# One graph-attention layer on one core: a quad's last gather issued first from the 17th quad on, carried rows added and divided later, and two operands moved between SBUF and PSUM

## The chip, the cores and the metric

The kernel runs on one core of one Trainium2 chip. The core has a tensor engine (PE, with its weight loads listed as PEld), a vector engine (DVE), a scalar engine (ACT), GpSimd (POOL, which also issues the indirect gathers) and a queue for plain transfers (SP). They run at the same time and wait for each other through semaphores. The time is the device time of one execution in microseconds; before the change it is 2001.82 us, the median of three runs (2001.02 to 2005.26).

## The reference

One layer of graph attention over 12500 nodes and 200000 edges, sorted by target node:

```
h = relu(layernorm(x)) @ W_node.T                      # 12500 x (4 heads x 32)
e = edge_attr @ W_edge.T                               # 200000 x (4 x 32)
att = leaky_relu(sum(concat(h[src], h[tgt], e) * a))   # one number per edge and head
m = max(segment_max(att, tgt), 0);  ex = exp(att - m[tgt])
denom = segment_sum(ex, tgt) + (num_edges - deg) * exp(-m)
out = x + segment_sum(ex / denom[tgt] * h[src], tgt)
```

Targets are skewed: many edges have a low target, few a high one, so equal numbers of edges cover few nodes at first and many later.

## The kernel before, in words

Edges are cut into 392 groups of 511, each held as four chunks of 128 rows with one place left over, chunk 0 row 0, for a sum carried in from the group before. Four groups are a quad (98 of them), and up to four quads a super. For each chunk POOL issues one indirect transfer (function `gather`, L180) that fetches 128 rows of 137 floats of a table of node values, made at the start, into the tile `ga`. `ga` holds eight quads, so the gathers of quad q overwrite the rows of quad q-8 and wait for its readers. There are 1566 gathers: 72 from the raw input at the start and 1494 from the table.

For each quad, `all_logits` compares targets with a range of nodes (DVE, tile `at`, L653 or L662), and multiplies edge features and target values into a bank `lg` (PE, L683 and L686). `add_sources` copies the sources' share out of the gathered rows (ACT, tile `U`, L730); it waits on a semaphore that counts the quad's gathers. Once a super is complete, `softmax` runs scans along its edges (DVE, L795 to L868, in the bank `t_ps`), which need a mask `kp` of edges that have the same target as the one before; `keeps` makes it on DVE (L763), from the targets `dr` and a copy of them that ACT puts into PSUM (L757, or L760 for the last super). Then `sums` goes over the quads one super behind: DVE multiplies `ga` by the weights (L1023, L1063) and marks rows in `hot` (L1006, L1065), and PE adds the rows up (L1093) into a bank `acc`, of which there are three.

Ranges of 4, 2 or 1 groups share one sum. For the first 75 quads (4 or 2), `passed_on` takes the last sum of the quad before along (DVE, L944, after an exponential on ACT, L938), `entered` adds carried rows into that quad's bank with a small matmul (PE, L963), and `settled` divides (`divide_ranges`, DVE, L1294 to L1303). From quad 75 on each group has its own sum: chunk 0 comes last, after the carried row (`carried_in`, ACT L916, PE L908), ACT copies the sum out (L976), and `divide` does it in SBUF (L1319 to L1333). The end of the program is an order by hand, `finale`: POOL takes over a few marks (L1002) and multiplications (L1023) once its gathers are issued, and one division is cut in two, the product (L1328) first and the addition of `x` (L1333) some steps later.

All engines keep the order in which this Python program records their instructions: generators advanced in turn (`together`, `chain`, `step`) write it, and nothing is moved by a scheduler. `checked` runs beside the sums: it looks whether the rows of targets are sorted, with four comparisons on DVE (L1467), each from SBUF and from a copy that ACT puts into PSUM (L1466).

Of the kernel before, what the change touches and what calls it, by code (L numbers as in the profile page):

```python
# [9 lines left out]
F32 = mybir.dt.float32  # L10
# [4 lines left out]
OP = mybir.AluOpType  # L15
# [54 lines left out]
def kernel(  # L70
# [100 lines left out]
    def gather(q, rows, width, lo, hi):  # L171

        g0, m = quads[q]
        ga = GA[q] = ga_all[:, q % QUADS]
        for i in range(lo, hi):
            n = -(-min(E - (g0 + i) * NE + 1, GE) // P)
            if n < J:
                nc.vector.memset(ga[:, i, n:, :], 0.0)
            for j in range(n):
                came = nc.gpsimd.indirect_dma_start(  # L180
                    out=ga[:, i, j, 0:width], out_offset=None, in_=rows,
                    in_offset=bass.IndirectOffsetOnAxis(ap=srci[:, g0 + i, j:j + 1], axis=0))
                if q >= QUADS:
                    came.then_inc(arrived[q % len(arrived)], 16)
                    tc.no_tile_sem_insts.add(came.ins.name)
                    tc.add_to_no_dep_group(f"rows{q}", came.ins)
                    landings[q] = landings.get(q, 0) + 16
# [354 lines left out]
    with tc.tile_pool(name="work", bufs=2) as work, \  # L542
# [52 lines left out]
        def fetch_windows(q):  # L595
# [5 lines left out]
                                rows_at(side, at[i], 2 * SIDE, span)) for i in range(n)]  # L601
# [146 lines left out]
        def keeps(s):  # L748
# [6 lines left out]
            if 0 < s < len(supers) - 1:  # L755
                before_ps = acc_pool.tile([P, GE], F32, name="acc")
# [172 lines left out]
        def passed_on(fc):  # L929
# [23 lines left out]
            state["passed"] = row, both, den[:1 + span, 0:n]  # L953

        def entered():
# [3 lines left out]
            (q, bank), (row, both, den) = state.pop("pending"), state.pop("passed")  # L959
# [76 lines left out]
        def sums(q):  # L1036
# [12 lines left out]
            k, span = class_of(q)  # L1049
            pt = work.tile([P, QG, ROW], F32, name="pt", bufs=3) if k == 1 else None  # L1050
# [21 lines left out]
            for i in range(m):  # L1072
# [10 lines left out]
                if not i:  # L1083
                    settled()
                if new:
# [4 lines left out]
                    fc = fac if g == s0 else None  # L1090
                least_j = 1 if k == 1 else 0
# [5 lines left out]
                if i == 1:  # L1097
                    passed_on(fac if g0 == s0 else None)
                if i == (2 if k > 1 else 1):
# [208 lines left out]
        def divide(q, pt, den, lo, hi, since, whole=True):  # L1308
# [16 lines left out]
            if not lo:  # L1325
                RES[q] = work.tile([P, QG, D], F32, name="res")
            res = RES[q][:R, lo:hi]
            nc.vector.tensor_tensor(  # L1328
                res[:, :n, :].rearrange("p g (h d) -> p g h d", d=HD), val[:, :, :, 0:HD],
                share_ps[0:R, :n, :].unsqueeze(3).to_broadcast([R, n, H, HD]), op=OP.mult)  # L1330

            def added():
                nc.vector.tensor_tensor(res[:, :n, :], res[:, :n, :], xw, op=OP.add)  # L1333
# [485 lines left out]
```

## Time and profile before

| | |
|---|---|
| median of 3 runs | 2001.82 us (2001.02 to 2005.26) |
| profiled execution | 2001.54 us, its span 1999.8 us |
| POOL | busy 1496.3 us (75%), of which 1566 gathers |
| DVE | busy 1199.0 us (60%) |
| PE / PEld | busy 1111.8 us (56%) / 762.8 us (38%) |
| ACT | busy 325.2 us (16%) |
| granted TensorE clock | 0.750 of full speed on average |
| HBM | 210.74 MB read, 17.43 MB written |

In the profile's rows a group stands as line, engine, operation, output<-input, then shapes and count; behind the bar its busy time and the mean of one in ns, then the idle time of the engine just ahead of it and what ended that. "issue" is time in which the engine waited for nothing that the profile shows. A row of the timeline begins with the start and the duration in us. A row of waits has the time in total, how often, and the longest.

### The profile page before, as it was taken

To read this page: it belongs to the slowest core of one execution; us is meant where nothing else is said; L and a number is where in the kernel's file an instruction comes from. 1 tells how busy PE (TensorE), PEld (TensorE's weight loads), DVE (VectorE), ACT (ScalarE), POOL (GpSimd) and SP (SyncE) were. 2 spreads that over 40 slices of the span, in tenths; PEclk is the share of its full clock that TensorE was granted. 3 is DMA by queue.
4 is the path that set the end of the run, shared out by engine and by line. 5 is a ranking of instruction groups with operands and counts; after the bars stand their busy time and mean duration, and the time that the engine had idled before them with its cause. 6 is when DMAs were issued, how large, how long until landed. Compare 5 with 4: busy or idle time off the path is not lost. (4 is left out here: it accounts for less than half of the span.)

```text
span 1999.8 us, 18826 instructions
## 1 busy us (share of the span) xinstructions
PE 1111.8 (56%) x5116; PEld 762.8 (38%) x5116; DVE 1199.0 (60%) x2695; ACT 325.2 (16%) x1081; POOL 1496.3 (75%) x1596
## 2 busy tenths in 40 slices
PE   6567676456364564554645635546446365465666
PEld 4445444334243342342433424424334233234344
DVE  8675888356265464563754735636547356366676
ACT  6564111001001010110010100100101011122222
POOL 7777777777777777777777777777777777777774
PEclk9788788677686776776867867768677667677777
DMA  7754755344343443444435434444354343434431
GB/s 253 207 134 98 175 134 137 75 107 109 97 111 91 119 108 96 114 104 117 118 85 130 115 90 118 106 115 118 86 127 109 85 119 98 122 98 115 111 98 40
DMA packets 167749, 229.58 MB, mean 115 GB/s; under 512 B 60827, under 2 KB 100669, under 8 KB 167638
## 3 DMA queue, kind: packets, MB, share of 16 engines
q0 software_dynamic: 50112, 109.61, 24.2%
q1 hardware_dynamic: 115824, 116.14, 20.4%
q10 hardware_dynamic: 1702, 2.59, 0.4%
q8 instruction: 41, 0.67, 0.1%
q14 instruction: 70, 0.57, 0.1%
HBM read 210.74 MB, written 17.43 MB: 114 GB/s over the span
## 5 line engine op out<-in xcount | busy, mean ns | idle before, releaser
L180 POOL DMA_INDIRECT ga<-table,srci x1494 | 1412.8, 946 | 457.0 <-issue 430.1
L1093 PEld LDWEIGHTS acc<-ga,hot 128*113 128x113 f32 (+1 forms) x2928 | 468.3, 207 | 548.7 <-issue 296.7
L1093 PE MATMUL acc<-ga,hot 128*113 128x137 f32 (+1 forms) x2928 | 528.6, 337 | 188.6 <-DVE hot L1065 43.6
L686 PE MATMUL lg<-at,pw 112*96 112x512 bf16 (+2 forms) x392 | 151.1, 423 | 247.0 <-DVE at L653 235.6
L683 PE MATMUL lg<-ea,by_pair 128*96 128x512 f32 (+1 forms) x392 | 243.1, 706 | 11.9 <-ACT tg L696 11.9
L653 DVE TENSOR_TENSOR at<-const_ps,db 112x1024 bf16<-112x1024 f32 (+1 forms) x176 | 212.5, 1208 | 6.1 <-DMA db<-offset 6.1
L763 DVE TENSOR_TENSOR kp<-dr,acc 64x512 f32<-64x512 int32 (+3 forms) x26 | 17.1, 659 | 300.5 <-ACT acc L757 300.5
L944 DVE SCALAR_TENSOR_TENSOR pt<-pt,spare,acc 1x133 f32<-1x133 f32 x113 | 38.0, 337 | 243.8 <-ACT den_of L938 242.4
L1063 DVE TENSOR_TENSOR ga<-ga,ex_ps 128x1056 f32<-128x1056 f32 x147 | 181.6, 1235 | 0.0
L787 PE MATMUL t_ps<-ident,U 128*64 128x128 f32 (+2 forms) x210 | 46.0, 389 | 216.3 <-ACT den_of L938 192.3
L730 ACT COPY U<-ga 128x64 f32<-128x64 f32 x98 | 29.0, 297 | 832.3 <-DMA ga<-table,srci 832.3
L1065 DVE TENSOR_TENSOR hot<-const_ps,slot 128x896 f32<-128x896 f32 (+1 forms) x147 | 143.3, 975 | 0.0
L787 PEld LDWEIGHTS t_ps<-ident,U 128*64 128x64 f32 (+2 forms) x210 | 36.5, 197 | 240.9 <-ACT den_of L938 208.3
L878 PE MATMUL ex_ps<-ident,stack 128*128 128x128 f32 x105 | 28.9, 428 | 156.4 <-DVE stack L868 138.7
L686 PEld LDWEIGHTS <-pw 112*96 112x96 bf16 (+2 forms) x392 | 53.8, 137 | 104.3 <-issue 100.4
L180 POOL DMA_INDIRECT ga<-in_x_dram,srci x72 | 68.3, 948 | 23.1 <-issue 18.6
L1023 DVE TENSOR_TENSOR ga<-ga,ex_ps 128x528 f32<-128x528 f32 x92 | 63.5, 693 | 36.4 <-ACT xs L884 36.3
L878 PEld LDWEIGHTS ex_ps<-ident,stack 128*128 128x128 f32 x105 | 18.6, 215 | 170.5 <-ACT stack L866 170.5
L683 PEld LDWEIGHTS lg<-ea,by_pair 128*96 128x96 f32 (+1 forms) x392 | 63.1, 192 | 34.3 <-issue 17.2
L712 PE MATMUL t_ps<-tg,of_head 96*64 96x512 f32 (+3 forms) x96 | 59.2, 703 | 3.4 <-ACT tg L696 3.4
L976 ACT COPY pt<-acc 81x137 f32<-81x137 f32 x88 | 23.7, 269 | 168.3 <-PE acc L908 166.2
L908 PE MATMUL acc<-ga,hot 128*81 128x137 f32 x176 | 44.4, 342 | 11.7 <-ACT ga L916 9.2
(204 smaller groups left out, 1278.3 us busy)
## 6 DMA issues: line engine op xcount, KB each, us to landing
ea<-in_edge_t_dram SPq DMA_DIRECT2D x196, 256.0 KB
ga<-table,srci POOLq DMA_INDIRECT x1494
db<-offset SPq DMA_DIRECT2D x53, 256.0 KB
db<-in_dst_dram SPq DMA_DIRECT2D x20, 320.0 KB
db<-offset SPq DMA_DIRECT2D x35, 160.0 KB
table<-row SPq DMA_DIRECT2D x9, 616.5 KB
xt<-in_x_dram SPq DMA_DIRECT2D x9, 576.0 KB
inputs<-in_x_dram SPq DMA_DIRECT2D x92, 56.0 KB
```

What stands on the lines that cost most here:

```text
L180: came = nc.gpsimd.indirect_dma_start(out=ga[:, i, j, 0:width], out_offset=None, in_=rows, in_offset=bass.IndirectOffsetOnAxis(ap=srci[:, ...
L653: nc.vector.tensor_tensor(AT[q][:span, i:i + n, :].rearrange("p g e -> p (g e)"), part_ps[:span].to_broadcast([span, n * GE]), DB[q][:span ...
L683: nc.tensor.matmul(lg, by_pair[:, begin:begin + n], ea[:, i // 2, :], start=half == 0 and i == 0, stop=False, skip_group_check=True)
L686: nc.tensor.matmul(lg, PW[q][:span, begin:begin + n], at[:span, i, :], start=False, stop=full and i == quads[q][1] - 1, skip_group_check=True)
L712: nc.tensor.matmul(TP[s][:groups(s)[1] * H], of_head[supers[s][1], p][:n], tg[:n], start=p == 0, stop=False, skip_group_check=True)
L787: nc.tensor.matmul(t_ps[:R, j * P:(j + 1) * P], u[:, j, :R], ident, start=False, stop=j == C - 1, skip_group_check=True)
L878: nc.tensor.transpose(turned_ps[:, j, :], stack[:, j * P:(j + 1) * P], ident)
L908: nc.tensor.matmul(acc, hot[:, i, 0, 0:acc.shape[0]], ga[:, i, 0, :], start=False, stop=stop)
L1023: engine.tensor_tensor(val, val, weight.unsqueeze(3).to_broadcast([P, J, H, HW]), op=OP.mult)
L1063: nc.vector.tensor_tensor(val, val, weight.unsqueeze(3).to_broadcast([P, TWO * J, H, HW]), op=OP.mult)
L1065: nc.vector.tensor_tensor(hot[:, i:i + TWO, :, 1:1 + span].rearrange("p g j c -> p (g j) c"), lane_ps[:, 0:span].unsqueeze(1).to_broadcast ...
L1093: nc.tensor.matmul(acc, hot[:, i, j, 0:1 + span], ga[:, i, j, :], start=new and j == J - 1 and not second, stop=k > 1 and i % k == k - 1 a ...
```

## The change

Eight edits, the line numbers below being those of the kernel before:

- `gather`: from quad 16 on, chunk 0 of the quad's last group is issued first, the others in the old order.
- `fetch_windows`: the weights of a quad are queued on SP from the last range to the first.
- `keeps`: the copy for the mask goes to the bank `t_ps`, no longer to one of the three `acc` banks; in `all_logits` a super of more than two quads makes its mask in its second quad, after the last group, where it was in its last quad, after the first group.
- `passed_on` and `entered`: from quad 8 to quad 74 the passing moves from after the second group to after the third; the division of the quad before stands right behind it (it was ahead of the first group), and the small matmuls stand ahead of the fourth group's matmuls (they were behind the third's).
- `divide`: where product and addition are apart (once, in `finale`), the product goes to the bank `lg` instead of the SBUF tile `res`.
- `checked`: the copy into PSUM is gone, and DVE compares two SBUF rows.

```diff
@@ gather
-        for i in range(lo, hi):
-            n = -(-min(E - (g0 + i) * NE + 1, GE) // P)
...
-            for j in range(n):
-                came = nc.gpsimd.indirect_dma_start(
...
+        order = [(i, j) for i in range(lo, hi) for j in range(chunks(i))]
+        if q >= 2 * QUADS:
+            order.sort(key=lambda at: at != (hi - 1, 0))
+        for i, j in order:
+            came = nc.gpsimd.indirect_dma_start(
...
@@ fetch_windows
-                                rows_at(side, at[i], 2 * SIDE, span)) for i in range(n)]
+                                rows_at(side, at[i], 2 * SIDE, span)) for i in range(n)[::-1]]
@@ keeps
-                before_ps = acc_pool.tile([P, GE], F32, name="acc")
+                before_ps = ps.tile([P, GE], F32, name="t_ps")
@@ passed_on / entered
-            state["passed"] = row, both, den[:1 + span, 0:n]
+            state["passed"] = state.pop("pending") + (row, both, den[:1 + span, 0:n])
...
-            (q, bank), (row, both, den) = state.pop("pending"), state.pop("passed")
+            q, bank, row, both, den = state.pop("passed")
@@ sums
+            later = k > 1 and q >= QUADS
...
-                if not i:
+                if not i and not later:
+                    entered()
                     settled()
...
+                if later and i == m - 1:
+                    entered()
...
-                if i == 1:
+                if i == (2 if later else 1):
                     passed_on(fac if g0 == s0 else None)
-                if i == (2 if k > 1 else 1):
+                    if later:
+                        settled()
+                if not later and i == (2 if k > 1 else 1):
                     entered()
@@ divide
+            product = res if whole else ps.tile([P, GE], F32, name="lg").rearrange(
+                "p (g d) -> p g d", d=D)[:R]
             nc.vector.tensor_tensor(
-                res[:, :n, :].rearrange("p g (h d) -> p g h d", d=HD), val[:, :, :, 0:HD],
+                product[:, :n, :].rearrange("p g (h d) -> p g h d", d=HD), val[:, :, :, 0:HD],
...
-                nc.vector.tensor_tensor(res[:, :n, :], res[:, :n, :], xw, op=OP.add)
+                nc.vector.tensor_tensor(res[:, :n, :], product[:, :n, :], xw, op=OP.add)
@@ all_logits
-                if i == 0 and q == sum(supers[of_quad[q]]) - 1 and q < first_fold:
+                q0, n = supers[of_quad[q]]
+                if i == (QG - 1 if n > 2 else 0) and q == q0 + min(1, n - 1) and q < first_fold:
                     keeps(of_quad[q])
@@ checked
-                rows_ps = acc_pool.tile([P, 512], F32, name="acc")[:n, 0:NE]
-                nc.scalar.copy(rows_ps, rows[:n, 0:NE])
-                nc.vector.tensor_tensor(falls[:n], rows[:n, 1:NE + 1], rows_ps, op=OP.is_lt)
+                nc.vector.tensor_tensor(falls[:n], rows[:n, 1:NE + 1], rows[:n, 0:NE],
+                                        op=OP.is_lt)
```

POOL around the end of quad 15 and the whole of quad 16, with the semaphores that each gather waits for (an engine's name is that engine's counter, DMASW that of an earlier gather), before:

```order
L180 DMA ga<-table,srci 128x137 [waits DMASW7_49]
L180 DMA ga<-table,srci 128x137 [waits DVE_49,PE_49,Activation_49]
L180 DMA ga<-table,srci 128x137 x3
L180 DMA ga<-table,srci 128x137 [waits DVE_49,PE_49]
L180 DMA ga<-table,srci 128x137 x3
```

and of the change, from the last four gathers of quad 15:

```order
L183 DMA ga<-table,srci 128x137 [waits DMASW4_49,DVE_49,PE_49]
L183 DMA ga<-table,srci 128x137 [waits DMASW5_49]
L183 DMA ga<-table,srci 128x137 [waits DMASW6_49]
L183 DMA ga<-table,srci 128x137 [waits DMASW7_49]
L183 DMA ga<-table,srci 128x137 [waits DVE_49,PE_49,Activation_49]
L183 DMA ga<-table,srci 128x137 x15
```

Before, the first gather of each group of four had waits of its own; now the first gather of the quad has them all, and fifteen follow without a wait.

PE in the middle of the program, at a quad with ranges of two groups (L1093 and L1100 are the sums, L963 and L966 the small matmuls that add carried rows, `lg` and `t_ps` the logits and selections of a later quad), before:

```order
L1093 MATMUL acc<-ga,hot 113x137 x4
L963 MATMUL acc<-pt,spare 2x133 x2
L683 MATMUL lg<-ea,by_pair 96x512
L686 LDWEIGHTS pw
L686 MATMUL lg<-at,pw 96x512
L712 MATMUL t_ps<-tg,of_head_0_102 64x512
L1093 MATMUL acc<-ga,hot 113x137 x4
```

and now:

```order
L1100 MATMUL acc<-ga,hot 113x137 x4
L686 MATMUL lg<-ea,by_pair 96x512
L689 LDWEIGHTS pw
L689 MATMUL lg<-at,pw 96x512
L715 MATMUL t_ps<-tg,of_head_0_102 64x512
L966 MATMUL acc<-pt,spare 2x133 x2
L1100 MATMUL acc<-ga,hot 113x137 x4
```

The two small matmuls went from behind the third group's sums, past the logits, to just ahead of the fourth group's.

DVE in `finale`, from the reciprocal of the cut division on, before:

```order
L1324 RECIPROCAL const_ps<-den 81x16
L1328 TENSOR_TENSOR res<-pt,const_ps 81x512
L883 MEMSET xs 128x4x8
L763 TENSOR_TENSOR kp<-dr,const_ps 64x129
L1023 TENSOR_TENSOR ga<-ga,ex_ps 128x4x132 x2
L918 TENSOR_TENSOR ga<-acc,fac 1x132
L1333 TENSOR_TENSOR res<-res,inputs 81x512
L795 TENSOR_TENSOR t_ps<-t_ps,low 64x128
```

and now:

```order
L1333 RECIPROCAL const_ps<-den 81x16
L1339 TENSOR_TENSOR lg<-pt,const_ps 81x512
L886 MEMSET xs 128x4x8
L766 TENSOR_TENSOR kp<-dr,const_ps 64x129
L1026 TENSOR_TENSOR ga<-ga,ex_ps 128x4x132 x2
L921 TENSOR_TENSOR ga<-acc,fac 1x132
L1344 TENSOR_TENSOR res<-lg,inputs 81x512
L798 TENSOR_TENSOR t_ps<-t_ps,low 64x128
```

The order is the same; the product now stands in PSUM (`lg`), and the addition reads one operand from there and one from SBUF, where it read two from SBUF.

19 lines of the change are left out of this document (10 added, 9 removed).

## The prediction

> **What bounds the kernel now.** I read the shares of the engines first, then what POOL waited for, then the last stretch engine by engine.
>
> ```profile
> PE 1111.8 (56%) x5116; PEld 762.8 (38%) x5116; DVE 1199.0 (60%) x2695; ACT 325.2 (16%) x1081; POOL 1496.3 (75%) x1596
> L180 POOL DMA_INDIRECT ga<-table,srci x1494 | 1412.8, 946 | 457.0 <-issue 430.1
> L180 POOL DMA_INDIRECT ga<-in_x_dram,srci x72 | 68.3, 948 | 23.1 <-issue 18.6
> POOL ga L180 <- issue: 448.7, 1471, 0.6
> POOL ga L180 <- PE acc L1093: 4.0, 13, 0.3
> ACT U L730 <- DMA ga<-table,srci: 832.3, 73, 19.4
> 3.00:1962.70 1959.70, 1089.40 (x4989) 743.48 (x4989) 1172.87 (x2609) 316.11 (x1040) 1481.08 (x1566) 0.75 0.46 117
> 1962.70:1999.80 37.10, 22.38 (x127) 19.33 (x127) 24.27 (x73) 9.12 (x41) 14.28 (x23) 0.73 0.09 22
> ```
>
> 75% looks like slack, but the idle time of POOL is issue time: 448.7 us over 1471 gaps is 0.305 us each, the longest 0.6. A gather takes 0.946 us, and 0.946 + 0.305 = 1.251; 1566 times that is 1959 us, the whole stretch from 3.0 to 1962.7 (the two window rows: length, then PE, PEld, DVE, ACT, POOL busy). So up to 1962.7 the time is a count of gathers, and everybody else waits: ACT alone stood 832.3 us before a quad's rows had landed. What can move the end is (a) a stall put into POOL's row of gathers, (b) a gather made longer, (c) the 37.1 us behind the last gather.
>
> **The change, part by part.**
>
> *Fewer waits on POOL, 0.* The gathers are as many. A gap ended by PE is 4.0/13 = 0.31 us, one by issue alone 0.305: the waits lie inside the gap. Even 0.005 us at each of the some 250 places that lose a wait would be 1 us. I take 0.
>
> *The new first gather waits for the last group of the quad eight before, 0.* Until now its own group, read first, was enough. The room left:
>
> ```profile
> 298.33 1.16 PE L1093 MATMUL acc<-ga,hot 128*81 128x137 f32 x8
> 325.55 0.94 POOL L180 DMA_INDIRECT ga<-table,srci  x1 [0.30 <-issue]
> 1035.38 1.10 PE L1093 MATMUL acc<-ga,hot 128*113 128x137 f32 x8
> 1084.55 0.94 POOL L180 DMA_INDIRECT ga<-table,srci  x1 [0.31 <-issue]
> ```
>
> Quad 8's last matmuls end at 299.5, quad 16's first gather goes out at 325.5: 26 us. In mid-program (quad 46, then quad 54) it is 1084.55 - 1036.48 = 48 us. The second pair is typical, the first the tightest of those reordered; no stall.
>
> *Carried rows later, division later, mask earlier, weights reversed: 0.* The same instructions in another order. The passing still stands on DVE behind ACT's exponential, which stands behind a copy `U` that waits for rows; queued behind it are DVE's weights and PE's fourth group. What covers that:
>
> ```profile
> 1164.50:1244.40 79.90, 41.98 (x192) 29.33 (x192) 45.12 (x85) 6.86 (x24) 60.39 (x65) 0.73 0.44 109
> DVE kp L763 <- ACT acc L757: 300.5, 23, 17.9
> DVE pt L944 <- ACT den_of L938: 242.4, 30, 13.6
> ```
>
> One super is 64 gathers, 79.9 us, in which DVE works 45 and PE 42. The 300.5 and 242.4 us that DVE stands before mask and passing are idle time of an engine that waits for gathers anyway; an earlier mask shortens that, and what is late next is again the gather. Without that cover the whole 543 us would count; with it none does. The edits end with quad 74 (mask and waits apart), 23 quads before the end, so they don't reach the last stretch.
>
> *Two SBUF operands in the sorting check, +0.6 us.* Four comparisons lose the copy in PSUM. A row of that kind, the addition L1333 next to the gathers:
>
> ```profile
> 1621.06 0.69 DVE L1333 TENSOR_TENSOR res<-res,inputs 81x512 f32<-81x512 f32 x1
> 1620.07 0.95 POOL L180 DMA_INDIRECT ga<-table,srci  x1 [0.30 <-issue]
> 1621.32 1.25 POOL L180 DMA_INDIRECT ga<-table,srci  x1 [0.30 <-issue]
> ```
>
> The gather beside it took 1.25 instead of 0.95: 0.3 us on the chain that sets the end. Not every one is hit, so I take half, 0.15 each, 0.6 in all; bounds 0 and 4 x 0.3 = 1.2. The Trainium skill ("SBUF — State Buffer", Who interferes with whom) infers that descriptor generation needs the write side of the port shared with GpSimd and a two-input operation only its read side. By that rule the term is 0 and the sum 0.6 lower; this row speaks for a small cost. The four copies saved on ACT are worth nothing (ACT is 16% busy).
>
> *The product in PSUM, in the last stretch, -2.8 us.* Here lies the one large number:
>
> ```profile
> 1966.90 0.27 DVE L918 TENSOR_TENSOR ga<-acc,fac 1x132 f32<-1x132 f32 x1
> 1967.10 5.35 DVE L1333 TENSOR_TENSOR res<-res,inputs 81x512 f32<-81x512 f32 x1
> 1972.38 0.28 DVE L795 TENSOR_TENSOR t_ps<-t_ps,low 64x128 f32<-64x128 f32 x1
> 1973.15 0.42 DVE L801 TENSOR_TENSOR_SCAN t_ps<-kp,t_ps 64x128 f32<-64x128 f32 x1
> 1973.90 0.21 DVE L806 COPY two<-t_ps 64x1 f32<-64x1 f32 x2 [0.32 <-ACT low L804]
> 1962.75 3.72 POOL L1002 TENSOR_SCALAR hot<-lane,slot 128x80 f32<-128x80 f32 x8
> 1966.45 5.28 POOL L1023 TENSOR_TENSOR ga<-ga,xe 128x528 f32<-128x528 f32 x5
> 1971.72 4.19 POOL L1002 TENSOR_SCALAR hot<-lane,slot 128x80 f32<-128x80 f32 x8
> 1966.61 0.27 ACT L792 ACTIVATE low<-t_ps 64x128 f32<-64x128 f32 x1 [0.94 <-PE t_ps L787]
> 1970.67 0.27 ACT L976 COPY pt<-acc 81x137 f32<-81x137 f32 x1 [3.26 <-PE acc L908]
> 1973.61 0.26 ACT L804 COPY low<-t_ps 64x128 f32<-64x128 f32 x1 [2.67 <-DVE t_ps L801]
> 1967.14 3.03 PE L1093 MATMUL acc<-ga,hot 128*81 128x137 f32 x12 [0.58 <-ACT ga L1034]
> 1969.97 0.67 PE L908 MATMUL acc<-ga,hot 128*81 128x137 f32 x2
> 1975.46 1.66 PE L1093 MATMUL acc<-ga,hot 128*81 128x137 f32 x6 [4.83 <-DVE ga L1023]
> ```
>
> The addition L1333 takes 0.69 elsewhere and 5.35 here, and it ends 0.7 after POOL's five multiplications, which also read two SBUF operands: DVE was shut out for all five, 4.66 us. L918 beside it, one operand from PSUM, took its 0.27. With `lg` in PSUM the addition takes 0.69 and L795, whose `low` was there at 1966.88, starts at 1967.8. But the 4.66 don't reach the end. The scans end 4.6 earlier, at 1968.9; next is ACT's copy L804, and on ACT it is queued behind L976, which waits for PE's L908 until 1970.64. L976 starts at 1970.67, and copies follow each other some 0.17 apart, so L804 runs at 1970.84 to 1971.1 and DVE's L806 at 1971.13 instead of 1973.90: **2.77 us**. From there the order stands as before: L806 leads to DVE's weights (L1023), these to PE at 1975.46, and on through the last softmax to the end; POOL's marks, over at some 1975.4, are not asked for in that stretch. So the term is -2.77. Bounds: -4.58 if ACT were not held by L976, and -2.3, if the small SBUF copies that now fall beside L1002 give back a whole mark of 3.72/8 = 0.47.
>
> **Sum:** -2.77 + 0.6 = -2.2. The profiled execution ran 2001.54 us around its span of 1999.8, which gives 1999.4; it stands 0.3 below the median shown, so on the median's scale **1999.6 us**, 0.1% less.
>
> **Rivals.**
>
> *Clock (faster, 1998.2).* PE stands idle for 4.83 us before 1975.46, and the next three batches run at half clock:
>
> ```profile
> 1960.93:1971.17 10.24, 6.66 (x26) 5.23 (x26) 9.68 (x16) 2.46 (x10) 9.90 (x15) 0.50 0.10 22
> 1971.17:1974.58 3.41, 0.00 (x0) 0.00 (x0) 2.95 (x8) 0.42 (x2) 3.41 (x7) 1.00 0.05 12
> 1974.58:1981.41 6.83, 5.38 (x23) 4.97 (x24) 5.67 (x29) 2.24 (x11) 1.97 (x4) 0.50 0.07 18
> ```
>
> The granted clock (third number from the end) was full just while PE had nothing to do, then half again. With PE back at 1972.7 the idle time is 2.1 us, and the clock may stay. The first batch, 1.66 + 0.67 us, would then halve, ACT's queue opens 1 us sooner, a later batch gives 0.4: -1.4 more. The Trainium skill ("TensorE: Matmul & The Clock Gate", What's actually happening) has the gate look at windows of about 3.4 us that run free of the program: the same lengths as these rows, and by it the phase, so luck, decides.
>
> *The stall only moves (no change, 2002.0).* Another chain of the last stretch, PE with ACT's carried copies, sets the end, or the sorting check takes its full 1.2. For it: PE is busy 22 of 37 us there. Against: its batches at 1975.46 start on DVE's word.
>
> *The reordered wait reaches POOL (slower).* One late group now holds all sixteen gathers. It decides once the sums fall 48 us behind, so once a quad takes longer than its 16 x 1.248 = 20.0 us on average. At 21 us, the 67 quads with later carries would lose 67 us, 48 of them hidden: +19, 2021 us. For it: the fourth group now waits for the passing, which waits for a later quad's rows. Against: DVE works 45 us of 80, and the lag settles at some 48 because gathers set it.
>
> **How the numbers follow.** The forecast, a gain of 1 to 3.4 us, has 0.60; the clock 0.14; no change 0.12; the stall on POOL 0.08; 0.06 stay for what I don't see, either way. A measurement can tell about 0.2%, 4 us: faster means under 1997.8. The forecast reaches that hardly ever (0.04), the clock's case every third time (0.05); with gains that I don't see and the 4 us spread of the runs, faster 0.20. Slower, over 2005.8: the stall and half of the rest, 0.11. Same 0.69. The range goes from 1996.8 (clock, and the upper bound of the tail) to 2003.0 (no change, all bounds against).
>
> **What would show it.** Right: gathers 1.248 apart with no gap over 0.6, the last one ending near 1963; the DVE addition from `lg` at 0.69 beside POOL's five multiplications; ACT's L804 straight behind its copy of `pt`; the rest 37.1 - 2.8 = 34.3 us long. DVE's waits for mask and passing smaller, and worth nothing. Wrong: gaps of several us between gathers, a tail as long as before, or one shorter by over 4.

## The result and the profile after

The changed kernel took 1999.17 us (median of 20 runs, 1996.88 to 2002.41) beside 2001.56 us (20 runs) of the kernel before: 0.9987 of it, 95% interval 0.9982 to 0.9993. So it is some 2.4 us faster, clear of zero, and less than the 0.2% that was called no change. Its profiled execution ran 2000.29 us around a span of 1998.4.

The first stage is where it was. Windows of the changed kernel, up to the end of the last gather and behind it:

```profile
3.00:1963.07 1960.07, 1123.94 (x4991) 760.81 (x4991) 1173.69 (x2613) 311.87 (x1038) 1481.57 (x1566) 0.73 0.47 117
1963.07:1998.40 35.33, 21.47 (x126) 18.33 (x125) 20.39 (x69) 8.79 (x40) 13.91 (x23) 0.74 0.10 22
```

and its waits (in total, how often, the longest; L183 is `gather`, was L180; L947 and L766 are the passing and the mask, were L944 and L763):

```profile
POOL ga L183 <- issue: 446.0, 1463, 0.6
DVE pt L947 <- ACT den_of L941: 516.5, 50, 15.3
DVE kp L766 <- ACT t_ps L760: 10.1, 6, 3.5
```

1566 gathers end at 1963.07 (1962.72 before, with a first gather at 3.26 instead of 3.03). No gap between two of them is over 0.6 us but one, of 1.4 us at the start of the table's gathers (104.93), which was 1.6 us long before. Behind the gathers lie 35.33 us instead of 37.10. DVE's wait for the mask fell from 300.5 to 10.1 us, and that for the passing rose from 242.4 + 15.4 to 516.5 + 15.4 (L950, its form for another range): together 558 before, 542 now. Most of the idle time changed its name.

The last stretch of the changed kernel, from the timeline (start, duration; numbers of the changed kernel: L1344 was L1333, L1026 was L1023, L979 was L976, L807 was L804, L1100 was L1093):

```profile
1966.78 0.67 DVE L1344 TENSOR_TENSOR res<-lg,inputs 81x512 f32<-81x512 f32 x1
1966.88 5.28 POOL L1026 TENSOR_TENSOR ga<-ga,xe 128x528 f32<-128x528 f32 x5
1967.72 3.03 PE L1100 MATMUL acc<-ga,hot 128*81 128x137 f32 x12 [0.58 <-ACT ga L1037]
1971.24 0.27 ACT L979 COPY pt<-acc 81x137 f32<-81x137 f32 x1 [3.40 <-PE acc L911]
1971.41 0.26 ACT L807 COPY low<-t_ps 64x128 f32<-64x128 f32 x1
1973.27 1.66 PE L1100 MATMUL acc<-ga,hot 128*81 128x137 f32 x6 [2.07 <-DVE ga L1026]
1991.67 0.56 DVE L1266 TENSOR_TENSOR res<-res,inputs 113x384 f32<-113x384 f32 x1
```

The addition takes 0.67 us in the middle of POOL's five multiplications (5.35 before), and ACT's copy `low` follows its copy of `pt` by 0.17. PE's next batch (1973.27) starts 10.2 us behind the last gather instead of 12.74: 2.55 us. In a second profile of the changed kernel, whose last gather ends at 1961.35, it starts at 11.4, and the gain there is 1.3 us:

```profile
1967.24 3.03 PE L1100 MATMUL acc<-ga,hot 128*81 128x137 f32 x12 [0.58 <-DVE ga L1026]
1972.79 1.66 PE L1100 MATMUL acc<-ga,hot 128*81 128x137 f32 x6 [2.07 <-DVE ga L1026]
```

In both profiles the next batch follows PE's batch of twelve matmuls, shown in the first row above, by 5.55 us. The prediction's chain, on the trace of before, gives the same distance: 1975.46 - 2.77 - 1967.14 = 5.55. What differs is where the batch of twelve stands: 4.6 and 5.9 us behind the last gather in the two profiles, 4.4 before. It hangs on ACT's copy `U`, which waits for the last rows in the first profile (it starts 3.0 us behind the last gather) but in the second stands in ACT's queue behind the softmax of the super before (4.3). With the addition held this makes no difference, as POOL's row starts 3.7 to 3.8 us behind the last gather in all three. The same last addition in the timeline of the kernel before:

```profile
1994.14 0.56 DVE L1257 TENSOR_TENSOR res<-res,inputs 113x384 f32<-113x384 f32 x1
```

It ended 32.0 us behind the last gather there, and 29.16 here: 2.8 us; in the second profile it was 30.6. The 0.3 us over 2.55 in the first of the two come from PE, whose clock is half until 1976.95 and full from then to 1994.00, so that one batch more ran at full speed. These are windows of the changed kernel, with the clock third from the end of a row:

```profile
1959.88:1976.95 17.07, 10.41 (x42) 8.76 (x42) 13.14 (x43) 3.70 (x16) 15.39 (x24) 0.50 0.12 27
1976.95:1994.00 17.05, 11.51 (x87) 9.86 (x85) 10.23 (x34) 5.52 (x25) 1.09 (x1) 1.00 0.09 21
```

The span fell by 1.4 us only, since from that addition's end to the span's end the last results took 6.2 us to leave in this execution and 5.1 in that of before; in a second profile of the changed kernel it was 4.2.

### The profile page after: what moved, and what is told of

It reads as the page before. It is cut to its first block, busy times and chain, and to the rows that moved or that the text cites. A ratio compares the mean times of both kernels' runs of the same rounds, so it can differ in the third digit from the quotient of the medians.

```text
span 1998.4 us, 18710 instructions
## 1 busy us (share of the span) xinstructions
PE 1145.4 (57%) x5116; PEld 779.1 (39%) x5116; DVE 1195.9 (60%) x2695; ACT 320.7 (16%) x1077; POOL 1496.4 (75%) x1596
## 5 line engine op out<-in xcount | busy, mean ns | idle before, releaser
L183 POOL DMA_INDIRECT ga<-table,srci x1494 | 1413.2, 946 | 456.6 <-issue 427.1
L1100 PE MATMUL acc<-ga,hot 128*113 128x137 f32 (+1 forms) x2928 | 544.7, 346 | 95.3 <-DVE hot L1009 55.2
L1100 PEld LDWEIGHTS acc<-ga,hot 128*113 128x113 f32 (+1 forms) x2928 | 484.5, 215 | 193.4 <-issue 80.2
L947 DVE SCALAR_TENSOR_TENSOR pt<-pt,spare,acc 1x133 f32<-1x133 f32 x113 | 38.3, 339 | 517.9 <-ACT den_of L941 516.5
L689 PE MATMUL lg<-at,pw 112*96 112x512 bf16 (+2 forms) x392 | 156.4, 435 | 271.7 <-DVE at L656 257.5
L686 PE MATMUL lg<-ea,by_pair 128*96 128x512 f32 (+1 forms) x392 | 230.8, 674 | 11.4 <-ACT tg L699 11.4
L881 PE MATMUL ex_ps<-ident,stack 128*128 128x128 f32 x105 | 28.8, 427 | 188.8 <-DVE stack L871 176.2
L881 PEld LDWEIGHTS ex_ps<-ident,stack 128*128 128x128 f32 x105 | 18.6, 215 | 202.9 <-ACT stack L869 202.9
L966 PEld LDWEIGHTS acc<-pt,spare 1*2 1x2 f32 x226 | 14.0, 86 | 207.9 <-issue 199.6
L183 POOL DMA_INDIRECT ga<-in_x_dram,srci x72 | 68.3, 949 | 23.3 <-issue 18.9
L1026 DVE TENSOR_TENSOR ga<-ga,ex_ps 128x528 f32<-128x528 f32 x92 | 63.5, 693 | 36.5 <-ACT xs L887 36.5
L699 ACT COPY tg<-lg 96x512 f32<-96x512 f32 (+1 forms) x51 | 29.6, 580 | 291.9 <-PE lg L689 275.0
L715 PE MATMUL t_ps<-tg,of_head 96*64 96x512 f32 (+3 forms) x96 | 71.0, 831 | 3.4 <-ACT tg L699 3.4
L715 PEld LDWEIGHTS t_ps<-tg,of_head 96*64 96x64 f32 (+3 forms) x96 | 11.8, 170 | 153.0 <-issue 146.8
```

The source lines that it names most:

```text
L183: came = nc.gpsimd.indirect_dma_start(out=ga[:, i, j, 0:width], out_offset=None, in_=rows, in_offset=bass.IndirectOffsetOnAxis(ap=srci[:, ...
L686: nc.tensor.matmul(lg, by_pair[:, begin:begin + n], ea[:, i // 2, :], start=half == 0 and i == 0, stop=False, skip_group_check=True)
L689: nc.tensor.matmul(lg, PW[q][:span, begin:begin + n], at[:span, i, :], start=False, stop=full and i == quads[q][1] - 1, skip_group_check=True)
L715: nc.tensor.matmul(TP[s][:groups(s)[1] * H], of_head[supers[s][1], p][:n], tg[:n], start=p == 0, stop=False, skip_group_check=True)
L881: nc.tensor.transpose(turned_ps[:, j, :], stack[:, j * P:(j + 1) * P], ident)
L947: nc.vector.scalar_tensor_tensor(to, row(w + at), passing[:, w + at:w + at + 1], own, op0=OP.mult, op1=OP.add)
```

## The experiments

Kernels that ran on one chip are compared with the kernel before on that chip; each time is given as a ratio to it, with its 95% interval. An interval is some 0.0009 to either side (1.8 us), so that most of the mechanisms below are read from the traces. A trace is of one execution, which need not be a typical one. The three columns on the right are counted in us from the end of the last gather: the start of PE's batch of twelve, the start of the batch behind it, and the end of DVE's last addition.

| run | ratio to before | last gather ends | batch of twelve | next batch | addition ends |
|---|---|---|---|---|---|
| before | | 1962.7 | 4.42 | 12.74 | 32.0 |
| changed kernel | 0.9987 (0.9982 to 0.9993) | 1963.1 | 4.64 | 10.19 | 29.2 |
| changed kernel, again | 0.9987 (0.9978 to 0.9996) | 1961.4 | 5.89 | 11.44 | 30.6 |
| before, product in `lg` alone | 0.9991 (0.9982 to 1.0000) | 1961.6 | 4.50 | 10.05 | 29.6 |
| changed, product in SBUF | 0.9998 (0.9989 to 1.0007) | 1963.0 | 3.69 | 12.75 | 31.8 |
| before, marks between | 0.9995 (0.9986 to 1.0004) | 1962.2 | 4.43 | 9.98 | 30.3 |
| changed, `low` ahead of `pt` | 0.9985 (0.9976 to 0.9994) | 1962.9 | 3.60 | 7.01 | 28.2 |
| ... and copy of `ends` moved | 0.9996 (0.9987 to 1.0005) | 1962.4 | 9.81 | 13.65 | 32.1 |
| ... and fifth group moved | 1.0006 (0.9997 to 1.0015) | 1961.5 | 9.80 | 13.67 | 33.3 |
| changed, reordered from quad 9 | 1.0008 (0.9999 to 1.0017) | 1965.9 | 5.91 | 11.47 | 30.6 |
| changed, all products in PSUM | 0.9993 (0.9984 to 1.0002) | 1960.1 | 6.93 | 12.21 | 32.4 |
| ... beside gathers only | 0.9991 (0.9982 to 1.0000) | 1960.3 | 5.45 | 11.00 | 30.0 |
| all products, and `low` ahead | 0.9990 (0.9981 to 0.9999) | 1961.0 | 7.80 | 11.08 | 33.2 |

### One edit alone, and all but that edit

```diff
+            product = res if whole else ps.tile([P, GE], F32, name="lg").rearrange(
+                "p (g d) -> p g d", d=D)[:R]
-                res[:, :n, :].rearrange("p g (h d) -> p g h d", d=HD), val[:, :, :, 0:HD],
+                product[:, :n, :].rearrange("p g (h d) -> p g h d", d=HD), val[:, :, :, 0:HD],
...
-                nc.vector.tensor_tensor(res[:, :n, :], res[:, :n, :], xw, op=OP.add)
+                nc.vector.tensor_tensor(res[:, :n, :], product[:, :n, :], xw, op=OP.add)
```

This was put into the kernel before, alone:

> The kernel before with one edit of the change alone: the product of the cut division goes to the PSUM bank lg. My theory: this edit is the whole gain. The addition takes 0.69 us instead of 5.35, the copy low L804 runs 8.3 us behind the last gather's end (10.9 before), DVE's last addition ends 2.5 to 2.8 us earlier, time 1999.2 us (-2.4). Rival, other edits share the gain (the waits taken off POOL, the comparisons, the order of the carries): less than half of it here, 2000.4 us or more.

and it was taken out of the changed kernel, with the other seven edits kept:

> The changed kernel with the product back in the SBUF tile res, all other edits kept. My theory: the other seven edits are worth nothing together, the addition takes 5.3 us again beside POOL's five multiplications, time 2001.5 us, the last gather ends where it does in both kernels (1962.7 to 1963.1). Rival, other edits share the gain: 2000.4 us or less, and then the gathers must end earlier.

The timeline of the kernel before with that edit:

```profile
1965.41 5.28 POOL L1023 TENSOR_TENSOR ga<-ga,xe 128x528 f32<-128x528 f32 x5
1966.23 0.67 DVE L1335 TENSOR_TENSOR res<-lg,inputs 81x512 f32<-81x512 f32 x1
1969.82 0.26 ACT L804 COPY low<-t_ps 64x128 f32<-64x128 f32 x1
```

and of the changed kernel without it:

```profile
1966.48 6.27 DVE L1342 TENSOR_TENSOR res<-res,inputs 81x512 f32<-81x512 f32 x1
1966.77 5.28 POOL L1026 TENSOR_TENSOR ga<-ga,xe 128x528 f32<-128x528 f32 x5
1973.90 0.26 ACT L807 COPY low<-t_ps 64x128 f32<-64x128 f32 x1 [3.41 <-DVE t_ps L804]
```

With the edit alone `low` starts 8.2 us behind the last gather (1961.62), without it at 10.9 (1963.02), and PE's next batch comes at 10.05 and at 12.75, as before, though the batch of twelve stood 0.7 us earlier in that run. Seven edits of eight are worth 0.9998 together, that is nothing that can be told from zero; none of the seven was run alone. The one alone gives 1.8 us by the medians (0.9991), 2.7 by PE's next batch and 2.4 by its addition's end. By the times alone the two kernels can't be told apart, as their intervals meet; it is the traces that put the gain on this edit. The 6.27 shows, too, that the addition is held though it begins 0.3 us ahead of POOL's first multiplication.

### What holds the addition

POOL's queue was changed in the kernel before: four marks between the second and the third multiplication.

```diff
             topped()
             step(older)
+            step(last_hot)
```

> The kernel before, where POOL makes four marks (one SBUF operand each) between its second and third multiplication (two SBUF operands each); product and addition stay in SBUF. My theory, DVE is shut out as long as POOL's two-operand instructions follow each other and gets in at the first instruction of another kind: the addition ends 2.1 + 0.7 us after the first multiplication's start, so takes some 2.3 us instead of 5.35, scans end 3 us earlier, ACT's copy L804 again behind its copy of pt, time 1999.1 us (-2.5). Rival 1, DVE waits until POOL's queue of multiplications is through, marks or not: the addition takes 7.2 us, time 2003.4 us. Rival 2, POOL isn't what holds the addition: 5.35 us as before, 2001.6 us.

Timeline of that kernel:

```profile
1965.92 2.13 POOL L1023 TENSOR_TENSOR ga<-ga,xe 128x528 f32<-128x528 f32 x2
1966.58 2.23 DVE L1333 TENSOR_TENSOR res<-res,inputs 81x512 f32<-81x512 f32 x1
1968.05 2.40 POOL L1002 TENSOR_SCALAR hot<-lane,slot 128x80 f32<-128x80 f32 x4
1970.31 0.26 ACT L804 COPY low<-t_ps 64x128 f32<-64x128 f32 x1
```

The addition, with both operands in SBUF as before, takes 2.23 us (2.3 expected) and ends 0.76 behind the second multiplication. So DVE is held by a row of two-operand instructions on POOL as a whole, and gets in at the first instruction of another kind. The four marks took 2.40 instead of 1.88; it is likely that the first of them waited for DVE. `low` came 8.1 behind the last gather and the next batch 5.55 behind the batch of twelve, as with the product in PSUM. Less of it arrived at the end (30.3), and the time (0.9995) can't be told from that of before; that the later multiplications (over at 1973.6) take the rest is likely and was not tried by itself.

### Whether ACT's queue set the size of the gain

The last softmax's scans and `low` were recorded ahead of the carry and the copy of `pt`. DVE's weights of the second group, now recorded by themselves, keep their place ahead of the scans; the addition moves behind them.

```diff
-            step(turned_last, turned_last, older, older)
-            added()
-            step(turned_last, turned_last, older)
+            step(turned_last, turned_last, older)
...
+            weighed(nc.vector, ga_all[:, (last - 2) % QUADS], 1,
...
+            AHEAD.add((last - 2, 1))
+            step(turned_last, turned_last, older, older)
+            added()
```

> The changed kernel with ACT's copy low L807 of the last softmax ahead of its copy of pt L979, instead of behind it (the scans are recorded one step earlier; the second group's multiplication by the weights keeps its place). My theory, the gain stopped at 2.6 us because L807 was queued behind L979, which waits for PE: L807 now runs some 5.9 us behind the last gather's end instead of 8.34, DVE's weights follow by 7.3, PE's next batch (10.20 in the changed kernel) starts right behind L911 at 8.2 to 8.4, and all behind it is 1.9 us earlier: 1997.3 us. Rival 1, the next chain (POOL's five multiplications, ACT's carried copies) holds PE by then: 1999.2 us. Rival 2, with the gap gone PE's clock stays full in one window more: up to 1996.0 us.

Timeline:

```profile
1966.67 5.28 POOL L1026 TENSOR_TENSOR ga<-ga,xe 128x528 f32<-128x528 f32 x5
1967.65 0.26 ACT L807 COPY low<-t_ps 64x128 f32<-64x128 f32 x1 [1.25 <-DVE t_ps L804]
1969.87 0.93 PE L1100 MATMUL acc<-ga,hot 128*81 128x137 f32 x6
1970.18 1.85 DVE L829 COPY ends<-tops 1x4 f32<-1x4 f32 x1
1975.77 0.30 PE L881 MATMUL ex_ps<-ident,stack 128*128 128x128 f32 x1 [3.28 <-ACT stack L869]
```

`low` starts 4.8 us behind the last gather and PE's batch at 7.0, 3.2 earlier than in the changed kernel's first profile. Of that, 1.0 lies ahead of the batch of twelve, since `U` had its rows 1.0 us sooner in this execution, and 2.1 are the edit's (3.41 instead of 5.55 behind that batch): ACT's queue was what stopped the gain, as the prediction had it. But the addition ends at 28.2, 0.9 earlier, not 1.9, and counted from the batch of twelve it ends 24.6 us behind it, where the changed kernel's two profiles have 24.5 and 24.7. The copy `ends` of four numbers, SBUF to SBUF, now falls among POOL's multiplications and stands 1.85 us, until their end at 1971.95; the scans hang on it, and PE's transposition L881 on them (3.28 us of waiting). PE's clock, full until then, fell as well: it is 0.51 of full from 1976.9 to 1980.3, where the changed kernel has full clock. So the 2.1 us were lost again on the way, and by the medians this kernel can't be told from the changed one.

### The copy moved ahead of the multiplications

The same kernel, with the copy and the clearing of `ends` recorded at the start of the last softmax (first diff), and then with the fifth group ahead of the transposition (second).

```diff
             if s == len(supers) - 1:
+                ends = turned.tile([1, 2, H, SBG + 1], F32, name="ends")
+                nc.vector.tensor_copy(ends[:, 0, :, 0], tops[:, :, s])
+                nc.vector.memset(ends[:, 1, :, m], 0.0)
                 yield
```

```diff
-            step(turned_last, older, turned_last)
+            step(turned_last, older, turned_last, older)
             together(turned_last)
             topped()
-            step(older)
```

> As the kernel with low ahead of pt, and besides the copy of tops into ends (SBUF to SBUF) and the clearing beside it are recorded before POOL's five multiplications begin, not among them. There the copy took 1.85 us instead of 0.16, and the transposition L881 on PE stood 3.3 us for what hangs on it. My theory, it is shut out by POOL like the addition was: without it the scans L832 follow the addition at 7.4 us behind the last gather, the next small copies can come after POOL's block (9.1), the transposition starts at 12.1 instead of 12.9, DVE's last addition ends at 27.5 instead of 28.2. Rival, the scans or the copies behind them are shut out in its place for as long: 28.2 again.

> As the run with the early copy of ends, and besides the fifth group of the two last quads' sums (PE's next batch) is recorded ahead of the last softmax's transposition instead of behind it. My theory, PE stands 9.6 to 12.1 with that batch ready, so the batch of 0.9 + 0.5 us comes for free: the last addition ends at 26.1 us behind the last gather, time 1995.3 (3.9 less than the changed kernel). Rival 1, the last softmax's chain by way of DVE's last three weights decides: 27.5. Rival 2, ACT's exponential queues behind the batch's copy and the transposition comes later: 28 or more.

Timeline of the first of the two:

```profile
1966.13 5.27 POOL L1030 TENSOR_TENSOR ga<-ga,xe 128x528 f32<-128x528 f32 x5
1966.77 0.28 DVE L766 TENSOR_TENSOR kp<-dr,const_ps 64x129 f32<-64x129 int32 x1 [0.25 <-ACT const_ps L763]
1966.97 4.47 DVE L785 COPY ends<-tops 1x4 f32<-1x4 f32 x1
1972.20 3.00 PE L1104 MATMUL acc<-ga,hot 128*81 128x137 f32 x12 [4.48 <-DVE ga L1030]
```

Both expectations failed on one slip of mine: in DVE's queue the new place lies behind the mask `kp`, which DVE reached at 1966.77, and POOL had begun at 1966.13. A copy of four numbers stood 4.47 us, DVE's two weights stood behind it, and PE's batch of twelve waited 4.48 for them: the addition ends at 32.1. In this execution the edit did the opposite of what was meant. In the second of the two kernels the copy stood 4.45 us as well, so that it says nothing on the fifth group.

Which of the two comes first is not fixed, though. In the changed kernel's second profile DVE reached the mask 0.65 us behind the start of POOL's row, as here:

```profile
1965.07 5.29 POOL L1026 TENSOR_TENSOR ga<-ga,xe 128x528 f32<-128x528 f32 x5
1965.72 0.28 DVE L766 TENSOR_TENSOR kp<-dr,const_ps 64x129 f32<-64x129 int32 x1 [0.25 <-ACT const_ps L763]
```

In its first profile it reached it 1.74 us ahead (1965.14, with POOL's row from 1966.88). The eleven times of the first of the two kernels fall into two groups that fit this: four from 1996.3 to 1997.2 us and seven from 1999.2 to 2002.5, and the profile is of the longest. The changed kernel beside it took 1998.06. It may be that the copy got in ahead of POOL in the four, and that the edit gains there; none of the four has a profile, so this is not shown.

### How much room the reordered gather needs

```diff
-        if q >= 2 * QUADS:
+        if q > QUADS:
```

> The changed kernel with the reordered first gather from quad 9 on instead of quad 16. The room there, last matmul of quad q-8 to first gather of quad q, is negative in the changed kernel's trace: -3.3 us at quad 9, -0.6 at 10, -4.9 at 12, then 7 or more. My theory, the new wait costs exactly where the room is missing: gaps of some 3.3 us before quad 9 and 1.6 more before quad 12, the last gather 4.9 us later, time 2004.0 us; if the sums get late by the same, up to 2007. Rival, the wait is absorbed since DVE and PE have idle time: 1999.2 us.

POOL's timeline at the first gathers of quad 9 and of quad 12:

```profile
188.70 0.94 POOL L183 DMA_INDIRECT ga<-table,srci  x1 [3.69 <-DVE into L842]
249.50 0.94 POOL L183 DMA_INDIRECT ga<-table,srci  x1 [1.13 <-ACT den_of L941]
```

At quad 9 the gap is 3.69 us, 3.39 above the usual 0.30 (3.3 expected); at quad 12 it is 0.83 above (1.6 expected). Between the hundredth and the 1200th gather the row got 4.2 us longer than in the changed kernel's first profile, and the last gather ended at 1965.85, where the two profiles of the changed kernel have 1963.1 and 1961.4. The kernel loses what it had won: 1.0008 instead of 0.9987, 4.2 us by the ratios. The new wait is thus a true one; it costs nothing in the changed kernel because 24 us or more are left at every quad from 16 on.

### Additions beside the gathers

```diff
-            product = res if whole else ps.tile([P, GE], F32, name="lg").rearrange(
-                "p (g d) -> p g d", d=D)[:R]
+            product = ps.tile([P, GE], F32, **({"name": "acc", "bufs": 3} if whole else {"name": "lg"})
+                              ).rearrange("p (g d) -> p g d", d=D)[:R]
```

> The changed kernel with the product of every undivided division (from quad 75 on) in a bank of acc as well, so that no addition of x has two SBUF operands any more while gathers run. My theory, the 2.05 us that gathers beside the 19 additions take above 0.944 each come from the two SBUF operands: the excess goes to under 0.2 us, the last gather ends 2.0 us earlier, tail as in the changed kernel, time 1997.2 us. Rival 1, a DVE instruction of 512 columns slows a gather wherever its operands lie: 1999.2 us. Rival 2, the bank taken from PE's three makes its sums late in the tail: slower than 1999.2.

In the second run the bank of `acc` was taken only while gathers run (`whole and "hold" not in state`), in the third the first form was joined with the edit of `low`:

> The changed kernel with the products in a bank of acc only while gathers run (to the second last super), in SBUF in the last stretch as in the changed kernel. With banks to the end the gathers were 3.0 us earlier, but ACT's last copy U came only 0.9 us earlier and the tail behind it lost more. My theory, the tail's part was the bank taken from PE there, the rest is DVE's wait for a bank ahead of the last super (40 us in sum): gathers end at some 1960.5, U at 1965.2, the last addition at 1991.3 on the profile's scale (1992.2 in the changed kernel), time 1998.3. Rival, with no wait in the tail the whole 2 us arrive: 1997.2.

> The changed kernel with both: the copy low ahead of the copy of pt, and every product in PSUM. If the two gains are of different stages they add: 2.0 in the gathers and 1.9 in the tail, 1995.3 us. If one of them is nothing, 1997.2 us; if the tail loses by the bank taken from PE, over 1996.

The first run's additions in the view by line (durations in ns, shortest, median and longest):

```profile
L1344 DVE TENSOR_TENSOR res<-acc,inputs x23: 420/686/687, 1623.7 to 1985.4; 81x512 f32<-81x512 f32 x19, 81x256 f32<-81x256 f32 x4
```

its waits, for the line of the products:

```profile
DVE acc L1339 <- ACT ga L919: 42.1, 8, 12.4
```

and its timeline, ACT's last copy `U` and a batch of PE in the last stretch:

```profile
1965.18 0.30 ACT L733 COPY U<-ga 128x64 f32<-128x64 f32 x1
1984.27 1.87 PE L1224 MATMUL acc<-ga,hot 128*81 128x137 f32 x14 [1.14 <-DVE res L1344]
```

and `U` in the changed kernel:

```profile
1966.10 0.30 ACT L733 COPY U<-ga 128x64 f32<-128x64 f32 x1 [0.99 <-DMA ga<-table,srci]
```

The stall of the gathers is gone: beside the 19 additions no gather took more than 0.95 us. In the changed kernel's first profile such gathers took 2.05 us above 0.944 in sum, the longest 1.38; in its second it was 0.97 us in sum. The last gather ended 3.0 us earlier than in the first and 1.3 earlier than in the second. But the time did not follow. `U` of the last quad, which opens the last stretch, stands 5.1 us behind the last gather now. It no longer waits for its rows but stands in ACT's queue behind the softmax of the super before, as it did in the changed kernel's second profile (4.3 behind). So it came only 0.9 and 0.45 us earlier than in the two. DVE waited 42.1 us for banks in this kernel, but about as much less for ACT's `low` between 1600 and 1962 (4.3 instead of 42.6), so that it is not shown that the banks made that softmax late. In the last stretch PE waits for banks that the additions hold (1.14 us at L1224, 1.1 more at two batches of L1100).

With the bank taken beside the gathers alone the addition ends at 30.0, or 1.9 us earlier by the clock of the span (1990.3 instead of 1992.2), which is what the rival said. But this profile is of the shortest of eleven executions, and by the medians on the same chip the kernel is 0.5 us ahead of the changed one, which can't be told from nothing. With both edits nothing adds: 33.2.

### All three together

The changed kernel with products in PSUM beside the gathers, `low` ahead of `pt`, and the copy of `ends` ahead of the cut division:

> The changed kernel with three further edits: the products in PSUM while gathers run, the copy low ahead of the copy of pt, and the small copy of ends recorded ahead of the cut division, so that DVE issues it before POOL's five multiplications begin (in the failed run DVE had reached it 0.85 us too late and stood 4.47 us). The copy takes at most one mark of POOL longer, under 0.7 us, and the scans behind follow the addition without a stall. If the gains of the single runs add: the last addition ends at 1988.6 us on the profile's scale (1990.3 with the products alone, less 0.9 for the order, less 0.75 for the copy), time 1996 us beside some 1998 to 1999 of the changed kernel and 2000.4 to 2001.6 of the one before. If the last stretch is bound elsewhere: the last addition at 1990.3, time as with the products alone, 1997.6.

This run came to a chip on which the kernel before took 2442.76 us as well, so it is compared with that alone: 2502.70, ratio 1.0252 (1.0231 to 1.0273). Its gathers are as long as elsewhere (0.947, then 0.30), but the first one of many quads waits:

```profile
1417.74 0.94 POOL L183 DMA_INDIRECT ga<-table,srci  x1 [3.95 <-ACT stack L875]
1441.26 0.94 POOL L183 DMA_INDIRECT ga<-table,srci  x1 [3.82 <-ACT tg L699]
```

From one of these gathers to the other, a quad, it is 23.5 us and not 20.0. The first gather of a quad has to wait, so the room of some 48 us is used up: this is the place that the slower rival named. What makes ACT and PE late on that chip the trace doesn't say (ACT's copy `tg` alone stood 541.7 us for a sender that isn't in the records), and the changed kernel itself was not run there. Whether the three gains add is open, and whether the reordering makes the 2.5% on such a chip as well.

## Why the prediction was right

1999.6 us were predicted and 1999.17 measured. Step by step:

- **What bounds it.** Right in the main. The row of gathers is 1959.7 us long before and 1959.8 in the changed kernel (3.03 to 1962.72, 3.26 to 1963.07), and the difference lies behind it. In the second profile of the changed kernel the row is 1958.2 us long, with the rest at 34.85, so a single profile is good for some 1.5 us here. And the gathers alone do not set where the last stretch begins: the softmax of the super before does so too, where it comes later.
- **Waits taken off POOL, 0; carries, division, mask and weights, 0.** Right in sum, to within the 1.8 us of the interval, by the run with all edits but one (0.9998). The batch of twelve stands 4.4 to 4.5 us behind the last gather in the three profiles without these edits, and 3.6 to 5.9 in those of the changed kernel, of the one with the product in SBUF and of the one with `low` ahead of `pt`; whether the edits do that was not tried. One sentence in it was wrong: that DVE's waits for mask and passing get smaller. Only the mask's did; the passing's took nearly all of it over, 558 to 542 us in sum. That fits the argument that what is late next is again the gather.
- **The reordered gather, 0.** Right, and for the reason given: the tightest room is 24 us in the changed kernel (26 were read from before), and where the room was missing the wait cost what was missing at quad 9 (3.39 us) and half of what was expected at quad 12 (0.83).
- **Two SBUF operands in the check, +0.6.** Too much: of the gathers beside the four comparisons one took 0.05 us longer (0.99 at 816.12), the others nothing. In the view by line the comparison itself is as long as the addition:

```profile
L1477 DVE TENSOR_TENSOR low<-rows x4: 672/674/678, 655.6 to 815.6; 128x511 f32<-128x511 int32 x3, 8x511 f32<-8x511 int32 x1
```

  The row taken as a model, the addition L1333, has two SBUF operands as well and the same length. What differs is where the next gather falls:

```profile
691.23 0.94 POOL L183 DMA_INDIRECT ga<-table,srci  x1 [0.30 <-issue]
691.37 0.68 DVE L1477 TENSOR_TENSOR low<-rows 128x511 f32<-128x511 int32 x1
815.62 0.67 DVE L1477 TENSOR_TENSOR low<-rows 8x511 f32<-8x511 int32 x1
816.12 0.99 POOL L183 DMA_INDIRECT ga<-table,srci  x1 [0.30 <-issue]
1908.82 0.69 DVE L1344 TENSOR_TENSOR res<-res,inputs 81x512 f32<-81x512 f32 x1
1908.94 1.38 POOL L183 DMA_INDIRECT ga<-table,srci  x1 [0.31 <-issue]
```

  Timeline of the changed kernel: first a gather that began 0.14 us ahead of a comparison, undisturbed; then one 0.50 us behind a comparison's start, longer by 0.05; last one 0.12 us behind an addition's start, longer by 0.43. How late the gather begins and how much longer it gets add up to 0.55 in both. In ten profiles with these additions in SBUF it is so throughout: all 78 gathers that began 0.07 to 0.53 us behind an addition's start got longer, delay and extra time adding up to 0.56 to 0.58 us, and no gather that began before it, or 0.56 us or more behind it, took over 0.955. The gathers behind the other three comparisons began 0.64, 1.10 and 1.14 us behind their starts, too late to be hit. If the start fell anywhere in the 1.25 us from gather to gather, an instruction would cost 0.13 us on average (an estimate, 0.56 x 0.56 / 2 / 1.25), near the 0.15 that was taken; the four simply fell well. That all-SBUF additions do lengthen gathers is shown by the run with the products in PSUM. The rule that the prediction named from the Trainium skill ("SBUF — State Buffer", Who interferes with whom), by which such an instruction leaves descriptor generation alone, gives the better number for the four comparisons and does not hold for these gathers beside the additions. They also read their row numbers from an SBUF tile (`srci`), and no run tells which of their accesses is held.
- **The product in PSUM, -2.77.** Right in mechanism: the addition is freed, and the next batch then follows the batch of twelve by the 5.55 us that the prediction's chain gives. The -2.77 takes for granted that the batch of twelve stays where it was. With the edit alone it nearly did, and the next batch came 2.7 us earlier; in the two profiles of the changed kernel it stood 0.2 and 1.5 us later, and the gain there was 2.55 and 1.3 us. That ACT's `pt` and not DVE was the stop is shown by the run with `low` ahead of it, where that batch followed 2.1 us sooner still.
- **The rest, 34.3.** It is 35.33 us in the first profile, because the last results took 1.1 us longer to leave, and 34.85 in the second.
- **Rivals.** The clock took part with about 0.3 us in the first profile of the changed kernel, one batch, and with under 0.1 in the second. The batch that the rival meant took 1.66 us as before, though PE stood idle only 2.07 us ahead of it. The stall did not merely move; the stall on POOL came only where it was forced, at quads 9 and 12, and on the chip of the last run.

That -2.2 met -2.4 so closely owes something to luck: the 0.55 us of the +0.6 that did not come, and what the product's term lost in one profile and not in the other, are less than two profiles of the changed kernel lie apart, 1.7 us in the end of the last gather and 1.5 the other way in the addition's end behind it.

## To carry to other kernels

Find the stage that really sets the end, and price an edit by its own queue there: 4.66 us taken off one DVE instruction were worth 1.3 to 2.7 at PE's next batch, because the next engine's queue had another waiter at its head. Beside a row of two-operand SBUF instructions on POOL, a DVE instruction with all its operands in SBUF, even a copy of four numbers, cost the rest of that row and everything queued behind it here; give it an operand in PSUM, or place it by the two queues' times, not by where the program text puts it. A stage relieved of 2 us gives them back where the next stage is paced by another chain. And read more than one execution: what starts a stage can differ between two executions of one kernel, here the last rows or the softmax before, and with it what an edit is worth, 2.55 and 1.3 us.

## What was not expected of the hardware

- A copy of 1x4 numbers from SBUF to SBUF on DVE took 4.47, 4.45 and 1.85 us among POOL's multiplications, and 0.16 as the median of the 28 in the changed kernel; an addition with one operand in PSUM took 0.67 among them. The Trainium skill ("SBUF — State Buffer", Who interferes with whom) lets such a copy contend, and gives the shared ports to one instruction at a time; here DVE's copy waited through all POOL instructions left of the row, and an addition got in where the marks began.
- Beginning first did not help: an addition that started 0.3 us ahead of POOL's first multiplication took 6.27 us (it ended 0.7 behind the fifth).
- A gather that starts within the first 0.56 us of an all-SBUF addition of 512 columns on DVE gets longer by what is left of these 0.56 us, by up to 0.43 us in the changed kernel; one that has started before it does not, nor one that starts later, though the addition runs for 0.69.
